# Four short-run transfers for the natural h, a new order of the first loads and constants, and a last norm by VectorE's statistics

## The chip, the cores and the metric

The kernel runs on one core of one Trainium2 chip. The metric is the device time of one execution in microseconds (us), lower is better. The names of the engines are those of the profile: PE is TensorE's matrix multiply, PEld its loading of weights (the stationary operand), DVE is VectorE, ACT is ScalarE, POOL is GpSimd, and SP is SyncE, the queue that issues nearly all DMA transfers here. All data is 32-bit float.

## What is computed

The input x holds 64 batches of 256 nodes with 128 channels; adj is a 256 x 256 symmetric-pattern matrix with values. Four graph layers follow each other; each one's result is added to its input and normalised over the channels.

```python
x = layernorm(x + chebyshev(x))            # layer 0: sum over k of A^k x W_k, k = 0..3, twice the same adj
x = layernorm(x + (adj @ (x @ W) + b))     # layer 1
x = layernorm(x + (A_norm @ x @ W.T + b))  # layer 2: A_norm = D^-1/2 (adj + I) D^-1/2
h = x
for step in range(5):                      # layer 3: a gated recurrent unit over the graph
    m = adj @ h                            # in_matrix and out_matrix are both adj here
    av = concat(m, m)
    u3 = h @ u3_w.T + u3_b
    z = sigmoid(av @ w3_w.T + w3_b + u3)
    r = sigmoid(av @ w4_w.T + w4_b + u3)
    hv = tanh(av @ w5_w.T + w5_b + ((r * h) @ u5_w.T + u5_b))
    h = (1 - z) * h + z * hv
x = layernorm(x + h)
```

## The kernel before

**Tiling.** The 64 batches are cut into 32 groups of two batches (`NB = 2`). One group's tensor is a tile of 128 partitions by 512 columns; its four node tiles (two batches of two tiles of 128 nodes) are the "q" of the code. A group runs through the four layers, and at most twelve groups are under way at once (`ACTIVE = 12`).

**Order.** Every piece of work is recorded as an `Op` with an engine, an assumed cost, a lag until others may use the result, and a rank. `Plan.order` simulates the engines with these figures and writes the instructions out in the order of the simulated start; an engine then runs its own list strictly in that order. Among pieces that could start at the same time the lower rank goes first. Pieces made by `pre` (loads, constants) have ranks written by hand; those of a group have the group's number as rank.

**Head.** `HEAD = 4`: groups that start below batch 4 (groups 0 and 1) are "near". A near group gets its transposed x by four PE transposes and one ACT copy (L867), multiplies by adj squared in the plain way (`propagate`, 8 PE instructions 256 columns wide) and uses `inner` (L584: 16 instructions of 256 columns, then 8 of 256). Every other group gets the transposed x by a DVE block transpose `tx` (L871), a store to DRAM and two loads back (L874, L879), uses `seven` (L723: seven block products instead of eight, 14 instructions of 128 columns, with sums and differences on POOL and DVE) and `inner_seven` (L618: 28 instructions of 128 columns, then 8 of 256). An fp32 product is two PE instructions.

**First loads and constants.** `a_nat` (adj), `w0_raw`, w1, and the six `raw_` weights are loaded on SP (L275, L306, L402, L407). PE transposes adj (L292), one ACT copy of 512 columns makes `aT` (L293), PE squares it, one ACT copy makes `a2T` (L303). The normalised adjacency `anT` comes by `degree`, a POOL power, `rows`, a PE transpose and `columns` (L369 to L373). `block_sums` (L378) makes five sums on DVE for each of `aT`, `a2T`, `anT` and `aTp`, where `aTp` is aT with its rows in another order (L345). From group 2 on, the load of a group's x waits for the first piece of work of the group two before it (`load_gate`, L956), until older gates take over.

**A step of layer 3** (L909 to L931). `seven` makes m from h with nodes on partitions ("natural"). PE then makes r, z and hv from m, from the transposed hT and from r * hT; ACT applies sigmoid and tanh; DVE makes the new hT. `packed` (L826) brings the natural h for the next step: one DVE block transpose (L830), one store of 256 KB to DRAM (L833) and two loads of 128 KB, one for each batch (L837). Its columns stand in pairs: the two node tiles' values for one channel lie side by side. `pairs` (L458) therefore gives `seven` a view with a stride of two elements, as PE's stationary operand and as POOL's input.

**End.** The last six batches (groups 29 to 31, `END = 6`) don't go through DRAM at the end: `closing` (L687) adds h and the residual in one PSUM bank, by products with `less` = I - 1/128 that also take out the mean. `spread_of` (L537) gets the mean square by four ACT squares with accumulation (L543), POOL takes the power -1/2 (L547), DVE multiplies (L704), and SP stores.

Of the kernel before, what the change touches and what calls it, by code (L numbers as in the profile page):

```python
# [14 lines left out]
P = 128  # L15
NB = 2
ACTIVE = 12
HEAD = 4
LEVEL = 7
# [158 lines left out]
def kernel(  # L178
# [105 lines left out]

    def flat(v):
        return v.ap.rearrange("p t n -> p (t n)")

    def turned_early():
# [3 lines left out]
    pre(-8, "PE", 8 * 110, turned_early, [a_nat], [p_at, warm])  # L292
    pre(-8, "ACT", act_cost(512), lambda: nc.scalar.copy(flat(aT), p_at.ap), [p_at], [aT])  # L293

# [7 lines left out]
    pre(-8, "PE", pe_cost(N, 4) + 220, square, [a_nat, aT], [p_a2, warm])  # L302
    pre(-8, "ACT", act_cost(512), lambda: nc.scalar.copy(flat(a2T), p_a2.ap), [p_a2], [a2T])  # L303

# [63 lines left out]

    pre(0.3, "DVE", 1500, degree, [a_nat], [ahat, deg])  # L369
    pre(0.3, "POOL", 700, lambda: nc.gpsimd.tensor_tensor(dinv.ap, deg.ap, half[:, :T], op=OP.pow), [deg], [dinv])  # L370
    pre(0.9, "DVE", 600, rows, [ahat, dinv, w0s], [ahat])
    pre(1.1, "PE", 4 * 110, lambda: turn(p_an, ahat), [ahat], [p_an])
    pre(0.3, "DVE", 900, columns, [p_an, dinv], [anT])  # L373

# [18 lines left out]
    block_sums(0.6, "a2T", a2T)  # L393
    block_sums(0.6, "anT", anT, (centred,))
    block_sums(0.7, "aTp", aTp, (centred,))

# [4 lines left out]
    made = pre(-7, "DVE", 100, lambda: nc.vector.tensor_copy(wb.ap[:, 1:3, 0], w0s.ap[:, :2, 0]), [w0s], [wb])  # L401
    fetch(0.6, wb.ap[:, 0, :], w1, wb, "SP")  # L402
    for i, b in ((1, b1), (2, b2)):
        last = fetch(0.5, wb.ap[:, i, :], bass.AP(tensor=b.tensor, offset=b.offset, ap=[[0, P], [1, C]]), wb, "POOL", (made,))
    pre(0.9, "DVE", 1100, lambda: centre(wb, wbm), [wb, w0s], [wb, wbm])
    w1c, b1c, b2c = ((wb, wb.ap[:, i, :]) for i in range(3))
    raw = {name: load(0.6, f"raw_{name}", [P, src.shape[1]], src, False, lag=9000)  # L407
           for name, src in (("w2", w2), ("w4", w4_w), ("w3", w3_w), ("w5", w5_w), ("u3", u3_w), ("u5", u5_w))}
    both = {name: Val("w", [P, C], f"both_{name}") for name in ("w4", "w3", "w5", "w34")}
    for name in ("w4", "w3", "w5"):  # L410
        pre(0.4, "DVE", 220, lambda o=both[name], i=raw[name]: nc.vector.tensor_add(  # L411
            o.ap, i.ap[:, :C], i.ap[:, C:]), [raw[name]], [both[name]])
    pre(0.4, "DVE", 220, lambda: nc.vector.tensor_sub(both["w34"].ap, both["w3"].ap, both["w4"].ap),
        [both["w3"], both["w4"]], [both["w34"]])
# [53 lines left out]
    class Group:  # L468
# [68 lines left out]
        def spread_of(self, tag, s):  # L537

            y, ve, rs = self.val("w", "y" + tag), self.val("ve", "ve" + tag), self.val("rs", "rs" + tag)

            def squares():
                for q in range(self.q):
                    nc.scalar.activation(nat(y)[:, q, :], nat(s)[:, q, :], AF.Square, scale=C ** -0.5,  # L543
                                         bias=root[:, 0:1], accum_out=ve.ap[:, q:q + 1])

            def scales():
                nc.gpsimd.tensor_tensor(rs.ap, ve.ap, half[:, :self.q], op=OP.pow)  # L547

            self.act(squares, [s], [y, ve], 390 * self.q)
            self.add("POOL", 1040, 100, scales, [ve], [rs])  # L550
            return y, rs

# [134 lines left out]
        def closing(self, y, hT, e, behind):  # L687
# [14 lines left out]
            self.pe(pe_cost(P, self.q), lambda: turned(e, False, True), [e, less], [s])  # L702
            o, rs = self.spread_of("3", s)
            self.dve(lambda: nc.vector.tensor_tensor(nat(o), nat(s), rs.ap[:, :, None].to_broadcast([P, self.q, C]),  # L704
# [121 lines left out]
        def packed(self, name, src):  # L826


            turn, far, t = self.val("w", "t" + name), self.val("dram", "d" + name), self.val("w", name)
            self.dve(lambda: nc.vector.transpose(  # L830
                turn.ap.rearrange("p (u j t) -> p u t j", t=T, j=32),
                src.ap.rearrange("p (u t i) -> p u t i", t=T, i=32)), [src], [turn])
            self.add("SP", 420, 2000, lambda: nc.sync.dma_start(far.ap, turn.ap), [turn], [far])  # L833

            def run():
                for b in range(self.nb):
                    nc.sync.dma_start(t.ap.rearrange("p (b r n) -> b p r n", b=self.nb, r=4)[b],  # L837
                                      far.ap.rearrange("(r i) (k b n) -> b (i k) r n", r=4, b=self.nb, k=4)[b])

            self.add("SP", 1000, 2300, run, [far], [t])  # L840
            return t
# [18 lines left out]
        def record(self):  # L860
            x_ = self.val("x", "x")
            plan.add("SP", 450, (6000, 9000)[self.start // NB] if self.start < HEAD else 2700, self.rank() - 1.5, lambda: nc.sync.dma_start(nat(x_), self.view(x)), [], [x_],
                     self.load_gate)
# [45 lines left out]
            for s in range(STEPS):  # L909
# [19 lines left out]
                if s < STEPS - 1:  # L929
                    hT = self.tensor(f"hT{s}", OP.add, hT, e)  # L930
                    h, ats, ins = self.packed(f"h{s}", hT), aTp, pairs  # L931
            if self.start < B - END:
# [13 lines left out]
    for i, nb in enumerate(sizes):  # L946
# [6 lines left out]
        if loaded:  # L953
            group.load_gate = (loaded[-1].last,)
        elif group.start >= HEAD:
            group.load_gate = (groups[i - 2].first,)  # L956
# [52 lines left out]
```

## Time and profile before

| | us |
|---|---|
| median of 3 runs (1341.92 to 1343.14) | 1342.21 |
| the profiled execution | 1342.32 |
| its span, first to last instruction | 1340.5 |
| PE busy | 1325.7 |
| DVE busy | 1039.0 |
| ACT busy | 773.6 |
| POOL busy | 636.1 |

The span is 1.8 us below the profiled execution's own time, and this execution stands 0.1 us above the median of the runs. Busy time is the union of an engine's instructions; since matmuls are pipelined and their ends are modelled, the rate of the PE is read from the distance of their starts, not from their durations. The granted TensorE clock is 0.997 of full speed on the mean over the span. "DMA" in the views by window is the mean busy share of the core's 16 DMA engines.

### The profile page before, as it was taken

What the parts mean: (1) busy time and instruction counts of PE and PEld (TensorE: products, weight loads), DVE (VectorE), ACT (ScalarE), POOL (GpSimd) and SP (SyncE); (2) the same over time, 40 slices, a digit from 0 to 9 for tenths busy, and PEclk for the clock granted to TensorE, in tenths of its full rate; (3) what the DMA queues carried; (4) which work ended last, traced back from release to release, by engine and by line L of the source; (5) the groups of instructions that cost most, each with busy time, mean ns of one, the idle gap of its engine ahead of it and who ended that gap; (6) DMA issues with size and microseconds to landing.
All of it is one profiled execution on the core that took longest, in us unless ns stands there. A gap on an engine that the chain in (4) does not pass through costs nothing.

```text
span 1340.5 us, 22669 instructions
## 1 busy us (share of the span) xinstructions
PE 1325.7 (99%) x6915; PEld 931.9 (70%) x6915; DVE 1039.0 (78%) x2577; ACT 773.6 (58%) x2361; POOL 636.1 (47%) x998
## 2 busy tenths in 40 slices
PE   8999999999999999999999999999999999999997
PEld 7987666667877766777766686777676776566554
DVE  7867767897778778788888797778876778777776
ACT  4587464645666664656655565655556786444445
POOL 5788352325646543447453454545345574232212
PEclk9999999999999999999999999999999999999999
DMA  7412333433433342333442343424322233333323
GB/s 190 131 33 79 88 95 87 141 107 96 115 95 111 95 121 70 110 95 103 121 124 74 108 134 87 119 71 119 101 73 68 60 111 103 112 109 95 89 85 103
DMA packets 269305, 134.87 MB, mean 101 GB/s; under 512 B 175712, under 2 KB 240864, under 8 KB 269184
## 3 DMA queue, kind: packets, MB, share of 16 engines
q1 hardware_dynamic: 268928, 133.29, 34.6%
q8 instruction: 55, 0.90, 0.3%
q0 software_dynamic: 256, 0.13, 0.1%
q14 instruction: 66, 0.54, 0.1%
HBM read 67.31 MB, written 65.80 MB: 99 GB/s over the span
## 4 chain that ended last, share of the span: by engine, by line
PE 97%; DVE 1%; DMA 1%; issue 0%; SPq 0%; ACT 0%; POOLq 0%; POOL 0%; ACTq 0%
PE pr L219 31%; PE ph L219 21%; PE pmg L219 19%; PE py L219 11%; PE pm L219 8%; PE pz L219 4%; PE pmq L219 3%; DMA x<-in_x_dram 1%; PE s L219 1%; DVE tx L871 0%; SPq L345 0%; DVE sd L635 0%; ACT y L543 0%; POOLq L1004 0%; DVE both_w L411 0%
## 5 line engine op out<-in xcount | busy, mean ns | idle before, releaser
L219 PE MATMUL pr<-mg,w435u5T 128*128 128x512 f32 x640 | 319.7, 593 | 0.0
L744 POOL TENSOR_TENSOR tsg<-h 128x256 f32<-128x256 f32 x128 | 94.0, 735 | 281.1 <-DMA h<-dh 200.4
L850 ACT ACTIVATE r<-pr,bsum 128x512 f32<-128x512 f32 x160 | 105.2, 658 | 123.4 <-PE pr L219 114.9
L850 ACT ACTIVATE pr<-pr,bsum 128x512 f32<-128x512 f32 x160 | 105.2, 658 | 118.0 <-PE pr L219 117.7
L547 POOL TENSOR_TENSOR rs<-ve,half 128x4 f32<-128x4 f32 x99 | 101.6, 1027 | 145.8 <-ACT y L543 137.2
L543 ACT ACTIVATE y<-s,root 128x128 f32<-128x128 f32 x396 | 153.7, 392 | 28.2 <-DVE s L565 25.5
L857 DVE TENSOR_TENSOR d<-ph,hT 128x512 f32<-128x512 f32 x160 | 109.6, 685 | 72.1 <-ACT ph L850 69.2
L219 PE MATMUL ph<-mg,w435u5T 128*128 128x512 f32 x320 | 163.3, 593 | 0.0
L219 PE MATMUL ph<-rh,w435u5T 128*128 128x512 f32 x320 | 162.7, 593 | 0.0
L219 PE MATMUL pr<-hT,w2u3T 128*128 128x512 f32 x320 | 162.2, 593 | 0.0
L219 PEld LDWEIGHTS pr<-mg,w435u5T 128*128 128x128 f32 x640 | 108.8, 191 | 70.3 <-issue 57.6
L850 ACT ACTIVATE ph<-ph,bsum 128x512 f32<-128x512 f32 x160 | 105.4, 659 | 57.8 <-PE ph L219 55.5
L219 PEld LDWEIGHTS pmg<-aTp,h 128*128 128x128 f32 x512 | 90.5, 196 | 64.8 <-issue 40.5
L857 DVE TENSOR_TENSOR rh<-r,hT 128x512 f32<-128x512 f32 x160 | 109.3, 683 | 33.1 <-ACT r L850 29.5
L558 ACT ACTIVATE y<-s,rs 128x128 f32<-128x128 f32 x384 | 122.1, 394 | 5.2 <-POOL rs L547 4.8
L857 DVE TENSOR_TENSOR pr<-pr,d 128x512 f32<-128x512 f32 x157 | 108.1, 691 | 1.7 <-ACT pr L850 0.5
L857 DVE TENSOR_TENSOR hT<-hT,pr 128x512 f32<-128x512 f32 x157 | 106.1, 678 | 1.3
L219 PE MATMUL pmg<-s_aTp,tsg 128*128 128x128 f32 x768 | 106.7, 275 | 0.0
L219 PEld LDWEIGHTS ph<-rh,w435u5T 128*128 128x128 f32 x320 | 58.5, 190 | 62.7 <-issue 46.2
L219 PE MATMUL pmg<-aTp,h 128*128 128x128 f32 x512 | 98.1, 279 | 0.0
L891 POOL TENSOR_TENSOR yb<-y,wb 128x512 f32<-128x512 f32 x64 | 81.7, 1277 | 34.3 <-ACT y L558 33.0
L780 DVE TENSOR_TENSOR mg<-pmg,usg 128x256 f32<-128x256 f32 x160 | 66.6, 418 | 39.7 <-PE pmg L219 38.3
(200 smaller groups left out, 2826.4 us busy)
## 6 DMA issues: line engine op xcount, KB each, us to landing
dh<-th SPq DMA_DIRECT2D x160, 256.0 KB, 2.0
h<-dh SPq DMA_DIRECT2D x256, 128.0 KB, 2.5
x<-in_x_dram SPq DMA_DIRECT2D x32, 256.0 KB, 3.2
hT<-dh SPq DMA_DIRECT2D x128, 64.0 KB, 2.1
out_dram<-y SPq DMA_DIRECT2D x32, 256.0 KB, 2.5
dx<-tx SPq DMA_DIRECT2D x30, 256.0 KB, 2.5
xT<-dx SPq DMA_DIRECT2D x60, 128.0 KB, 2.7
dn<-tn SPq DMA_DIRECT2D x29, 256.0 KB, 2.0
```

What stands on the lines that cost most here:

```text
L219: nc.tensor.matmul(o, lhsT, rhs, start=start, stop=stop, skip_group_check=shared)
L543: nc.scalar.activation(nat(y)[:, q, :], nat(s)[:, q, :], AF.Square, scale=C ** -0.5, bias=root[:, 0:1], accum_out=ve.ap[:, q:q + 1])
L547: nc.gpsimd.tensor_tensor(rs.ap, ve.ap, half[:, :self.q], op=OP.pow)
L558: nc.scalar.mul(nat(y)[:, q, :], nat(s)[:, q, :], rs.ap[:, q:q + 1])
L744: nc.gpsimd.tensor_tensor(ts.ap[:, :2 * P].rearrange("p (x c) -> p x c", x=2), ins(h)[:, 1], ins(h)[:, :, 0], op=OP.subtract)
L780: nc.vector.tensor_tensor(o(m, slice(1, 3)), o(ps, slice(1, 3), False), both, op=OP.add)
L850: self.act(lambda: nc.scalar.activation(t.ap, ps.ap, func, bias=bias[1], scale=1.0), [ps, bias[0]], [t], act_cost(self.width) + 100)
L857: self.dve(lambda: nc.vector.tensor_tensor(out(t), way(a), way(b), op=op), [a, b], [t])
L891: nc.gpsimd.tensor_tensor(nat(yb), nat(y), bias[1][:, None, :].to_broadcast([P, self.q, C]), op=OP.add)
```

## The change

The natural h of steps 1 to 4 is laid out with each node tile contiguous. The DVE transpose keeps plain 32-blocks, and `packed` loads by four transfers (one for each node tile q) with runs of 32 elements, 128 bytes, where it had two with runs of 64 elements. `seven` then gets `ins = None`, the contiguous view `tiles`.

`HEAD` becomes 6, so that group 2 is near too. The loads of x for groups 2 and 3 lose their gate, and have other assumed lags. The copies to `aT` and `a2T` are halved between ACT and DVE. `degree`, the power, `rows`, the turn, `columns`, the sums of `anT` and `aTp`, w1, the raw weights and the sums of w3, w4 and w5 get ranks from 1.9 to 2.6, where they had 0.3 to 1.1; `degree` now waits for `w0s`.

The last group (batches 62 and 63) gets its mean square by DVE: four `bn_stats`, four `bn_aggr` and one add, in place of the four ACT squares.

```diff
--- before.py
+++ after.py
@@ -15,7 +15,7 @@
 P = 128
 NB = 2
 ACTIVE = 12
-HEAD = 4
+HEAD = 6
 LEVEL = 7
 PLAIN = 0
 END = 6
@@ -282,15 +282,17 @@
                 nc.tensor.transpose(ps.ap[:, mt * N + nt * P:mt * N + (nt + 1) * P],
                                     src.ap[:, nt, mt * P:(mt + 1) * P], ident)
 
-    def flat(v):
-        return v.ap.rearrange("p t n -> p (t n)")
-
     def turned_early():
         turn(p_at, a_nat)
         warming(4)
 
     pre(-8, "PE", 8 * 110, turned_early, [a_nat], [p_at, warm])
-    pre(-8, "ACT", act_cost(512), lambda: nc.scalar.copy(flat(aT), p_at.ap), [p_at], [aT])
+    def halved(v, ps):
+
+        pre(-8, "ACT", act_cost(N), lambda: nc.scalar.copy(v.ap[:, 0, :], ps.ap[:, :N]), [ps], [v], joint=True)
+        pre(-8, "DVE", 420, lambda: nc.vector.tensor_copy(v.ap[:, 1, :], ps.ap[:, N:]), [ps], [v], joint=True)
+
+    halved(aT, p_at)
 
     def square():
         for mt in range(T):
@@ -300,7 +302,7 @@
         warming(2)
 
     pre(-8, "PE", pe_cost(N, 4) + 220, square, [a_nat, aT], [p_a2, warm])
-    pre(-8, "ACT", act_cost(512), lambda: nc.scalar.copy(flat(a2T), p_a2.ap), [p_a2], [a2T])
+    halved(a2T, p_a2)
 
 
     w0_raw = load(-1, "w0_raw", [P, C, K0], w0, lag=7300)
@@ -366,11 +368,11 @@
             nc.vector.tensor_scalar(anT.ap[:, mt, :], p_an.ap[:, mt * N:(mt + 1) * N], dinv.ap[:, mt:mt + 1],
                                     None, op0=OP.mult)
 
-    pre(0.3, "DVE", 1500, degree, [a_nat], [ahat, deg])
-    pre(0.3, "POOL", 700, lambda: nc.gpsimd.tensor_tensor(dinv.ap, deg.ap, half[:, :T], op=OP.pow), [deg], [dinv])
-    pre(0.9, "DVE", 600, rows, [ahat, dinv, w0s], [ahat])
-    pre(1.1, "PE", 4 * 110, lambda: turn(p_an, ahat), [ahat], [p_an])
-    pre(0.3, "DVE", 900, columns, [p_an, dinv], [anT])
+    pre(2.3, "DVE", 1700, degree, [a_nat, w0s], [ahat, deg])
+    pre(2.3, "POOL", 720, lambda: nc.gpsimd.tensor_tensor(dinv.ap, deg.ap, half[:, :T], op=OP.pow), [deg], [dinv])
+    pre(2.3, "DVE", 800, rows, [ahat, dinv], [ahat])
+    pre(2.3, "PE", 4 * 110, lambda: turn(p_an, ahat), [ahat], [p_an])
+    pre(2.3, "DVE", 900, columns, [p_an, dinv], [anT])
 
 
     sums_of = {}
@@ -391,26 +393,26 @@
 
     block_sums(0.6, "aT", aT)
     block_sums(0.6, "a2T", a2T)
-    block_sums(0.6, "anT", anT, (centred,))
-    block_sums(0.7, "aTp", aTp, (centred,))
+    block_sums(2.4, "anT", anT, (centred,))
+    block_sums(2.6, "aTp", aTp, (centred,))
 
 
 
     wb, wbm = constant("wb", [P, 3, C]), constant("wbm", [P, 3])
 
     made = pre(-7, "DVE", 100, lambda: nc.vector.tensor_copy(wb.ap[:, 1:3, 0], w0s.ap[:, :2, 0]), [w0s], [wb])
-    fetch(0.6, wb.ap[:, 0, :], w1, wb, "SP")
+    fetch(1.9, wb.ap[:, 0, :], w1, wb, "SP")
     for i, b in ((1, b1), (2, b2)):
         last = fetch(0.5, wb.ap[:, i, :], bass.AP(tensor=b.tensor, offset=b.offset, ap=[[0, P], [1, C]]), wb, "POOL", (made,))
     pre(0.9, "DVE", 1100, lambda: centre(wb, wbm), [wb, w0s], [wb, wbm])
     w1c, b1c, b2c = ((wb, wb.ap[:, i, :]) for i in range(3))
-    raw = {name: load(0.6, f"raw_{name}", [P, src.shape[1]], src, False, lag=9000)
+    raw = {name: load(2.0, f"raw_{name}", [P, src.shape[1]], src, False, lag=9000)
            for name, src in (("w2", w2), ("w4", w4_w), ("w3", w3_w), ("w5", w5_w), ("u3", u3_w), ("u5", u5_w))}
     both = {name: Val("w", [P, C], f"both_{name}") for name in ("w4", "w3", "w5", "w34")}
     for name in ("w4", "w3", "w5"):
-        pre(0.4, "DVE", 220, lambda o=both[name], i=raw[name]: nc.vector.tensor_add(
+        pre(2.0, "DVE", 300, lambda o=both[name], i=raw[name]: nc.vector.tensor_add(
             o.ap, i.ap[:, :C], i.ap[:, C:]), [raw[name]], [both[name]])
-    pre(0.4, "DVE", 220, lambda: nc.vector.tensor_sub(both["w34"].ap, both["w3"].ap, both["w4"].ap),
+    pre(2.0, "DVE", 300, lambda: nc.vector.tensor_sub(both["w34"].ap, both["w3"].ap, both["w4"].ap),
         [both["w3"], both["w4"]], [both["w34"]])
 
     less = constant("less", [P, P])
@@ -548,6 +550,23 @@
 
             self.act(squares, [s], [y, ve], 390 * self.q)
             self.add("POOL", 1040, 100, scales, [ve], [rs])
+            return y, rs
+
+        def spread_at_once(self, tag, s):
+
+            st, mv, ve, rs, y = (self.val(k, n + tag) for k, n in (
+                ("st", "st"), ("mv", "mv"), ("ve", "ve"), ("rs", "rs"), ("w", "y")))
+
+            def stats():
+                for q in range(self.q):
+                    nc.vector.bn_stats(st.ap[:, q * 6:(q + 1) * 6], nat(s)[:, q, :])
+                for q in range(self.q):
+                    nc.vector.bn_aggr(mv.ap[:, 2 * q:2 * q + 2], st.ap[:, q * 6:(q + 1) * 6])
+                nc.vector.tensor_scalar(ve.ap, mv.ap.rearrange("p (q k) -> p k q", k=2)[:, 1], EPS, None, op0=OP.add)
+
+            self.dve(stats, [s], [st, mv, ve], 260 * self.q + 110)
+            self.add("POOL", 1040, 100, lambda: nc.gpsimd.tensor_tensor(rs.ap, ve.ap, half[:, :self.q], op=OP.pow),
+                     [ve], [rs])
             return y, rs
 
         def normalise_centred(self, tag, s):
@@ -700,7 +719,7 @@
 
             self.pe(pe_cost(P, self.q) + pe_cost(self.width), early, [hc, y, less], [s], behind=(behind,))
             self.pe(pe_cost(P, self.q), lambda: turned(e, False, True), [e, less], [s])
-            o, rs = self.spread_of("3", s)
+            o, rs = (self.spread_at_once if self.start >= B - NB else self.spread_of)("3", s)
             self.dve(lambda: nc.vector.tensor_tensor(nat(o), nat(s), rs.ap[:, :, None].to_broadcast([P, self.q, C]),
                                                      op=OP.mult), [s, rs], [o])
             return o
@@ -827,17 +846,17 @@
 
 
             turn, far, t = self.val("w", "t" + name), self.val("dram", "d" + name), self.val("w", name)
-            self.dve(lambda: nc.vector.transpose(
-                turn.ap.rearrange("p (u j t) -> p u t j", t=T, j=32),
-                src.ap.rearrange("p (u t i) -> p u t i", t=T, i=32)), [src], [turn])
+            self.dve(lambda: nc.vector.transpose(turn.ap.rearrange("p (u j) -> p u j", j=32),
+                                                 src.ap.rearrange("p (u i) -> p u i", i=32)), [src], [turn])
             self.add("SP", 420, 2000, lambda: nc.sync.dma_start(far.ap, turn.ap), [turn], [far])
 
             def run():
-                for b in range(self.nb):
-                    nc.sync.dma_start(t.ap.rearrange("p (b r n) -> b p r n", b=self.nb, r=4)[b],
-                                      far.ap.rearrange("(r i) (k b n) -> b (i k) r n", r=4, b=self.nb, k=4)[b])
-
-            self.add("SP", 1000, 2300, run, [far], [t])
+                f = far.ap.rearrange("(r i) (k q j) -> q (i k) r j", r=4, q=self.q, k=4)
+                o = t.ap.rearrange("p (q r j) -> q p r j", q=self.q, r=4)
+                for q in range(self.q):
+                    nc.sync.dma_start(o[q], f[q])
+
+            self.add("SP", 450 * self.q, 2300, run, [far], [t])
             return t
 
         def product(self, ps, w, rhs, start, stop, shared=False):
@@ -859,7 +878,7 @@
 
         def record(self):
             x_ = self.val("x", "x")
-            plan.add("SP", 450, (6000, 9000)[self.start // NB] if self.start < HEAD else 2700, self.rank() - 1.5, lambda: nc.sync.dma_start(nat(x_), self.view(x)), [], [x_],
+            plan.add("SP", 450, dict(zip(range(0, 4 * NB, NB), (6000, 9000, 10500, 9000))).get(self.start, 2700), self.rank() - 1.5, lambda: nc.sync.dma_start(nat(x_), self.view(x)), [], [x_],
                      self.load_gate)
 
             near = self.start < HEAD
@@ -928,7 +947,7 @@
                 e = self.tensor(f"e{s}", OP.mult, z, d, into=pr)
                 if s < STEPS - 1:
                     hT = self.tensor(f"hT{s}", OP.add, hT, e)
-                    h, ats, ins = self.packed(f"h{s}", hT), aTp, pairs
+                    h, ats, ins = self.packed(f"h{s}", hT), aTp, None
             if self.start < B - END:
                 hT = self.tensor("hT", OP.add, hT, e)
                 hn = self.brought("hn", self.turned("n", hT, "p (k q i) -> p q k i", "p (k q j) -> p q k j"))
@@ -952,7 +971,7 @@
             group.gate = (done[-1].last,)
         if loaded:
             group.load_gate = (loaded[-1].last,)
-        elif group.start >= HEAD:
+        elif group.start >= 4 * NB:
             group.load_gate = (groups[i - 2].first,)
         group.record()
         groups.append(group)
```

## The prediction

> **What bounds the kernel now.** I read the page first: which engine is full, and what the transfers cost.
>
> ```profile
> PE 1325.7 (99%) x6915; PEld 931.9 (70%) x6915; DVE 1039.0 (78%) x2577; ACT 773.6 (58%) x2361; POOL 636.1 (47%) x998
> ...
> q1 hardware_dynamic: 268928, 133.29, 34.6%
> ...
> h<-dh SPq DMA_DIRECT2D x256, 128.0 KB, 2.5
> ...
> hn<-dn SPq DMA_DIRECT2D x116, 64.0 KB, 2.0
> ```
>
> PE is busy for all but 15 us of a span of 1340.5; DVE, ACT, POOL and the DMA engines have room. So time is saved only by less PE work, faster PE work, or fewer of those 15 us. The busy time by windows shows where they lie (columns: window, then busy us and instructions of PE, PEld, DVE, ACT, POOL, then granted clock, DMA share, GB/s).
>
> ```profile
> 25.00:30.00 5.00, 2.95 (x25) 2.72 (x23) 3.58 (x7) 3.42 (x15) 4.44 (x7) 1.00 0.93 255
> 30.00:35.00 5.00, 1.93 (x9) 1.93 (x10) 4.83 (x12) 0.68 (x3) 1.26 (x2) 0.61 0.82 230
> 35.00:40.00 5.00, 4.64 (x31) 4.35 (x31) 3.44 (x12) 1.98 (x8) 0.87 (x1) 0.71 0.76 204
> 40.00:50.00 10.00, 8.98 (x73) 8.59 (x72) 9.20 (x23) 3.86 (x16) 7.89 (x13) 1.00 0.02 4
> 50.00:60.00 10.00, 10.00 (x83) 9.73 (x83) 9.38 (x23) 7.93 (x34) 8.31 (x12) 1.00 0.90 254
> ...
> 120.00:600.00 480.00, 480.00 (x2451) 329.99 (x2450) 372.53 (x917) 271.72 (x802) 221.84 (x353) 1.00 0.35 101
> ```
>
> PE idles 2.05 + 3.07 + 0.36 + 1.02 = 6.5 us between 25 and 50, and never from 50 to 1330. The clock column adds a second loss: after the stall PE runs at about half speed from 33.07 to 38.0, where it is busy 1.93 + 2.64 = 4.6 us; half of that, 2.3 us, is lost. The hole is worth 8.8 us. The rest is start-up (PE begins real work at 4 us) and the 7 us after the last matmul. PE's waits (who waited for whom: us in total, times, longest) and then DVE's timeline (start us, duration us, instruction, idle before) name the cause.
>
> ```profile
> PE pmq L219 <- DVE mq L776: 5.1, 1, 5.1
> ...
> PE pz L219 <- DVE u L664: 1.0, 1, 1.0
> ```
>
> These and two waits at 1.4 and 0.4 us are all that PE has in the whole run. What DVE did meanwhile:
>
> ```profile
> 26.11 1.13 DVE L871 STREAM_TRANSPOSE tx<-x 128x512 f32<-128x512 f32 x1 [1.79 <-DMA x<-in_x_dram]
> 27.17 0.82 DVE L366 TENSOR_SCALAR anT<-p_an,dinv 128x256 f32<-128x256 f32 x2
> 28.27 1.08 DVE L871 STREAM_TRANSPOSE tx<-x 128x512 f32<-128x512 f32 x1 [0.28 <-DMA x<-in_x_dram]
> ...
> 29.77 1.65 DVE L385 TENSOR_TENSOR s_anT<-anT 128x128 f32<-128x128 f32 x1
> ...
> 31.67 0.28 DVE L770 TENSOR_TENSOR usq<-usq,pmq 128x128 f32<-128x128 f32 x1
> ```
>
> DVE works in order. From 24.3 it waits for a gated x, then transposes two x, makes anT and its sums, and only at 31.67 reaches the short additions for group 2's `pmq`, whose last product PE can't write before. Early constants and late x stand ahead of what PE needs.
>
> **What the Trainium skill says.** "TensorE: Matmul & The Clock Gate", section "What's actually happening": an idle window of about 3.4 us throttles the PE clock to half, and it takes about as long of work to come back. The trace agrees: 5.1 us idle, then 0.61 and 0.71 granted. The same page, "LDWEIGHTS (loading the stationary operand)", gives columns / 1.2, 107 ns for 128; the trace's products of 128 columns start 111.7 ns apart, so these are bound by their loads. "SBUF — State Buffer", "Door 1: The DMA port swizzle", says that an fp32 stride up to a 16-byte line is free; a stride of two elements should then cost nothing. The trace differs (PE timeline):
>
> ```profile
> 1267.45 0.40 PE L219 MATMUL pmg<-aTp,h 128*128 128x128 f32 x2
> 1267.68 0.83 PE L219 MATMUL pmg<-s_aTp,tsg 128*128 128x128 f32 x6
> 1268.35 0.40 PE L219 MATMUL pmg<-aTp,h 128*128 128x128 f32 x2
> ```
>
> The strided h takes 0.23 / 2 = 115 ns for each, the contiguous tsg 0.67 / 6 = 112. Over 60 to 1300 us the starts in the trace lie 115.4 ns apart on the mean after a strided h, 111.7 after tsg or tqg. The measurement decides: 3.7 ns for each.
>
> **The change part by part.**
>
> (a) *Contiguous h as weights.* The groups pmg<-aTp,h (x512) and pmg<-s_aTp,h (x256) are 768 products in steps 1 to 4. 768 x 3.7 ns = **-2.8 us**, all on PE and so all on the path. Bounds: 0 if the difference isn't the stride's; -4.6 if the 6 ns between the medians of the durations (281 against 275) counts. POOL gains nothing: its first difference takes 732 ns from strided h and 731 from contiguous y. Nor does the DVE transpose: 704 ns in `packed`, 702 and 704 in `turned`, which moves whole blocks.
>
> (b) *Four transfers for two.* 128 x 2 more issues on SP at about 0.45 us each: 115 us more on a queue that now issues some 860 transfers (390 us, 29% of the span), giving 38%. SP has room, but h comes later: two issues take 0.91 us, the four of `hn` 1.75, so +0.84 us for each step. From issue to POOL's use is 3.0 us now (1278.40 to 1281.38), and a step's chain is some 17.5 us: POOL 1.9, `seven` about 3, two ACT gates 1.3, six DVE pieces 4.1, PE in between 1.7, store 2.3, loads 3.0. Two groups of PE work, 2 x 6.6 us, cover 13 of this, three cover 20; up to twelve are under way, so it is hidden but for the last steps. I take 0, and 0 to +2 as bounds for the end. Packets: 131072 of 256 bytes become 262144 of 128. The trace's records give 17.9 ns on the mean for a 256-byte packet. "DMA: Bandwidth & Descriptors", "Why small descriptors are slow (HBM only)", has 3 cycles on top of one for 32 bytes, 11 for 256 bytes and 7 for 128: estimate 11.4 ns each, which the trace doesn't show. The DMA engines then get 40 us more each (the share 38%), at most 147 us (46%) if a packet costs the same. No bound either way.
>
> (c) *Group 2 near.* PE gets more work: four transposes, 4 x 0.112 = 0.45; `propagate` 8 x 0.216 against 14 x 0.112, +0.16; `inner` 24 x 0.216 = 5.18 against 28 x 0.112 + 8 x 0.216 = 4.86, +0.32. Sum **+0.9 us**, certain. (0.216 is the distance of the starts of 256-column products.) It takes `tx`, its store and two loads, the differences and the short additions off POOL, DVE and SP: on DVE 1.1 + 1.7 + 1.1 + 1.6 = 5.5 us, just where DVE is late. And PE gets 7.3 us of work that needs only ACT.
>
> (d) *Order of loads and constants.* x of groups 2 and 3 now goes out ungated after the fourth SP issue, at about 3 to 4 us, ahead of aTp, w1 and the raw weights (now 10.4 us and later). Group 3's tx can run at about 10 us instead of 20.8; DVE then doesn't meet a missing x. w1 and the six raws issue behind aTp, about 11 to 14 us, land 4 to 5 us later; the first use of w1 is near 25 us, later for the others. DVE gives up about 1.6 us of `degree` before 5.4 us and some 9 us of anT, its and aTp's sums and the raw sums between 12 and 32; they come back beside groups 0 to 3, where `inner` needs no DVE. PE's supply from 8.5 us: three near groups, 3 x 7.3 = 22 us, so to about 31; then group 3 (6.4) and layer 1 of groups 0 to 2 (2.5 each), to about 45. DVE must do in 15 to 45 some 8 us of constants, 17 for three DMA groups, 5 for layer 1: 30 of 30 us. It just fits, so I don't take the whole hole: of 8.8 us I take **-7.0**, with 1.8 left as short waits without a cold clock. Bounds: 0 and -8.8.
>
> (e) *Halved copies.* An ACT copy of 512 columns takes 0.59 us, of 256 0.37; a DVE piece from PSUM of 256 columns 0.41 to 0.42. DVE is free at both places once `degree` is gone. 2 x 0.17 = **-0.3**, if x and w0s don't hold PE instead (w0s was done at 12.9, behind the sums of a2T).
>
> (f) *The last norm.* The tail's timeline:
>
> ```profile
> 1331.61 1.95 PE L219 MATMUL s<-less,e 128*128 128x128 f32 x16
> ...
> 1334.29 1.01 POOL L547 TENSOR_TENSOR rs<-ve,half 128x4 f32<-128x4 f32 x1 [3.50 <-ACT y L543]
> ...
> 1335.69 1.01 POOL L547 TENSOR_TENSOR rs<-ve,half 128x4 f32<-128x4 f32 x1 [0.39 <-ACT y L543]
> ```
>
> ACT squares group 30 until 1334.2 and group 31 until 1335.6. DVE would start group 31 at 1333.6: four bn_stats 0.87 (start of the first to end of the last, L519), four bn_aggr 0.4, the add 0.17: ready at 1335.0. POOL is then taken by group 30's power until 1335.3, so the second starts 0.35 us earlier: **-0.35**. If bn_stats from PSUM costs 0.07 more each, still -0.3; bounds 0 and -0.4.
>
> Sum: -2.8 + 0 + 0.9 - 7.0 - 0.3 - 0.35 = -9.5. 1342.3 - 9.5 = 1332.8, against the profiled execution's 1342.32, which is the runs' median within 0.1.
>
> **The rivals.**
>
> *The hole moves instead of closing.* The constants that are put later meet DVE, POOL and SP at 25 to 50 us, where DVE was already 92% busy in 40 to 50. For it: DVE's 30 of 30. Against it: from 50 to 120 us DVE carried 72 to 94% and PE waited for nothing. If only a quarter of the hole goes, -2.2 for -7.0: 1337.6.
>
> *Slower, by late h.* Each of 128 steps has 0.84 us more between store and use. For it: the h issued at 1278.40 has its last difference ready at 1283.18, and PE takes its first product at 1283.22, with no slack. Against it: POOL waits 200 us in all for h, and PE waits for nothing after 50 us. The gains must be eaten first: 9.5 + 2.7 for slower by 0.2%, that is 12.2 / 0.84, about 15 of 128 steps with the whole delay on PE, most likely in the last three groups' four steps each plus gaps that the clock makes dearer. At 16 steps: 1332.8 + 13.4 = 1346.2.
>
> *The stride isn't the cause* of the 3.7 ns: (a) is nothing and the time is 1335.6. This lies inside the forecast's range.
>
> **How the numbers follow.** Forecast (hole mostly closed, with or without the stride's gain) 0.70, the moved hole 0.18, late h 0.12. The forecast's own range is 1329.5 (the whole hole, a stride at 4.6) to 1336. 0.2% of 1342 is 2.7 us, about what a measurement can tell from no change: faster below 1339.5, slower above 1344.9. Faster: 0.70 + 0.14 of the moved hole = 0.84; same: 0.04 of it and 0.02 of the late h, 0.06; slower 0.10. The range for 8 in 10 must take in most of the moved hole: 1329 to 1339.
>
> **What would show it.** (a): medians of the pmg<-aTp,h loads at 192 ns and matmuls at 275, starts 112 apart. (b): h<-dh x512 of 64 KB, packets near 400,000, and PE's waits from 50 to 1330 still near nothing. (c): twelve `ptx` transposes where there are eight, and 24 products of 256 columns on `pmq<-a2T,x` where there are 16. (d): no PE wait over 2 us between 25 and 50 and a clock of 1.00 there. (e): p_a square starting about 0.2 us after p_at less than now. (f): the last power on POOL right behind the one before. A wait of PE on DMA-fed POOL work after 1250 us, or a throttled window, would prove me wrong.

## The result and the profile after

The changed kernel takes 1335.93 us (median of 5 runs, 1335.43 to 1336.32) where the kernel before takes 1342.21 (5 runs beside them): ratio 0.9952, 95% interval 0.9939 to 0.9966, 6.3 us less. The profiled execution took 1335.43 with a span of 1333.5; 6.9 us below the profiled execution of before, of which the steps are counted here. The forecast was 1332.8, inside the range of 1329 to 1339 and the right way, but with half as much gain again as there was (9.5 for 6.3).

The page after, engines, queue and the loads of h:

```profile
PE 1321.0 (99%) x6901; PEld 925.1 (69%) x6901; DVE 1037.3 (78%) x2574; ACT 774.3 (58%) x2355; POOL 632.7 (47%) x995
...
q1 hardware_dynamic: 402896, 132.78, 39.5%
...
h<-dh SPq DMA_DIRECT2D x512, 64.0 KB, 2.4
```

There are 134,000 packets more for the same bytes, and the DMA share is up from 34.6 to 39.5%: inside the bounds of 38 and 46%. PE still bounds the kernel. Busy time by windows after (columns as before):

```profile
25.00:30.00 5.00, 5.00 (x30) 4.51 (x29) 2.56 (x3) 3.85 (x17) 4.17 (x6) 1.00 0.83 233
30.00:35.00 5.00, 4.94 (x37) 4.55 (x35) 4.18 (x6) 4.06 (x16) 3.18 (x5) 1.00 0.90 236
35.00:40.00 5.00, 2.78 (x21) 2.50 (x22) 5.00 (x17) 2.53 (x10) 3.91 (x6) 1.00 0.89 240
40.00:50.00 10.00, 9.15 (x82) 8.99 (x81) 9.20 (x28) 5.19 (x24) 8.48 (x13) 1.00 0.61 162
50.00:60.00 10.00, 9.79 (x80) 9.42 (x80) 10.00 (x27) 4.86 (x22) 8.69 (x13) 1.00 0.30 79
...
120.00:600.00 480.00, 479.51 (x2479) 330.43 (x2478) 387.35 (x950) 279.17 (x836) 225.50 (x355) 1.00 0.42 105
```

The 5 us hole at 28 to 33 is gone, and so is the half clock behind it: it reads 1.00 in each of these windows. A smaller hole stands at 35 to 38. PE's waits and DVE's timeline after name it:

```profile
PE pmq L219 <- ACT usq L805: 1.9, 1, 1.9
...
PE pm L219 <- DVE m L795: 1.2, 2, 0.8
PE pmg L219 <- DVE mg L795: 0.5, 1, 0.5
```

```profile
30.23 1.11 DVE L890 STREAM_TRANSPOSE tx<-x 128x512 f32<-128x512 f32 x1 [2.12 <-DMA x<-in_x_dram]
31.27 0.82 DVE L368 TENSOR_SCALAR anT<-p_an,dinv 128x256 f32<-128x256 f32 x2
32.65 1.12 DVE L890 STREAM_TRANSPOSE tx<-x 128x512 f32<-128x512 f32 x1 [0.56 <-DMA x<-in_x_dram]
33.71 1.13 DVE L385 TENSOR_TENSOR s_anT<-anT 128x128 f32<-128x128 f32 x1
34.87 0.70 DVE L386 TENSOR_TENSOR s_anT<-s_anT,anT 128x128 f32<-128x128 f32 x1
...
36.03 0.27 DVE L789 TENSOR_TENSOR us<-us,pm 128x128 f32<-128x128 f32 x1
```

It is the same picture as before, some 4 us later and with the x of later groups: DVE waits for a late x, transposes it, makes anT and its sums, and only at 36.03 reaches the short addition. Two of the sums take 1.13 and 0.70 us where their like takes 0.28; POOL's additions run beside them. ACT's copy of `usq` stands behind ACT's `m`, which comes only after that addition, and PE waits for the copy. PE's timeline after shows the products on h:

```profile
1260.72 0.39 PE L219 MATMUL pmg<-aTp,h 128*128 128x128 f32 x2
1260.94 0.83 PE L219 MATMUL pmg<-s_aTp,tsg 128*128 128x128 f32 x6
1261.61 0.39 PE L219 MATMUL pmg<-aTp,h 128*128 128x128 f32 x2
```

Two products on h now take 0.22 us from start to start and not 0.23: the mean over all 768 is 111.0 ns, where it was 115.4. The tail after:

```profile
1328.33 1.01 POOL L568 TENSOR_TENSOR rs<-ve,half 128x4 f32<-128x4 f32 x1
1328.39 0.69 DVE L723 TENSOR_TENSOR y<-s,rs 128x512 f32<-128x512 f32 x1 [0.36 <-POOL rs L549]
1329.11 1.35 SPq L958 DMA_DIRECT2D out_dram<-y  x2
1329.37 0.69 DVE L723 TENSOR_TENSOR y<-s,rs 128x512 f32<-128x512 f32 x1 [0.28 <-POOL rs L568]
```

The last product starts at 1326.35 and the last power 1.98 us later, where it was 2.40 (1333.29 and 1335.69).

### The profile page after: what moved, and what is told of

It is laid out like the page before. It is cut to its first block, busy times and chain, and to the rows that moved or that the text cites. A ratio compares the mean times of both kernels' runs of the same rounds, so it can differ in the third digit from the quotient of the medians.

```text
span 1333.5 us, 23248 instructions
## 1 busy us (share of the span) xinstructions
PE 1321.0 (99%) x6901; PEld 925.1 (69%) x6901; DVE 1037.3 (78%) x2574; ACT 774.3 (58%) x2355; POOL 632.7 (47%) x995
## 3 DMA queue, kind: packets, MB, share of 16 engines
q1 hardware_dynamic: 402896, 132.78, 39.5%
## 4 chain that ended last, share of the span: by engine, by line
PE 96%; DVE 3%; DMA 1%; ACT 0%; issue 0%; POOL 0%; POOLq 0%; DVEq 0%; ACTq 0%; SPq 0%
PE pr L219 31%; PE ph L219 20%; PE pmg L219 19%; PE py L219 11%; PE pm L219 7%; PE pz L219 4%; PE pmq L219 3%; DMA x<-in_x_dram 1%; PE s L219 1%; DVE tx L890 0%; PE warm L270 0%; ACT y L545 0%; DVE se L660 0%; DVE sf L663 0%; DVE sd L654 0%
## 5 line engine op out<-in xcount | busy, mean ns | idle before, releaser
L219 PEld LDWEIGHTS pmg<-aTp,h 128*128 128x128 f32 x512 | 86.7, 191 | 60.7 <-issue 38.4
L219 PEld LDWEIGHTS pmg<-s_aTp,tsg 128*128 128x128 f32 x768 | 96.0, 192 | 0.0
```

The lines of the kernel that those rows point to most:

```text
L219: nc.tensor.matmul(o, lhsT, rhs, start=start, stop=stop, skip_group_check=shared)
```

## The experiments

Each kernel was run in five rounds beside the kernel before, whose median was 1342.3 to 1342.7. "Lost" is worked out from the traces: the sum, over PE's products, of the distance to the next start less 112, 216 or 430 ns for 128, 256 or 512 columns. After 120 us only gaps of more than 0.03 us over that are counted, so the stride isn't in it. Before, e2_split and e3_tail have the same order and the same front, and differ by 0.9 us at 25 to 80 and by nothing after 120: smaller differences in the third column mean nothing.

| kernel | ratio to before, 95% interval | lost at 25 to 80 us | lost after 120 us |
|---|---|---|---|
| before | 1 | 9.6 | 0.7 |
| changed | 0.9952 (0.9939 to 0.9966) | 4.7 | 0.9 |
| e1_layout | 0.9988 (0.9981 to 0.9994) | 9.8 | 1.9 |
| e2_split | 1.0005 (0.9997 to 1.0014) | 9.9 | 0.7 |
| e3_tail | 0.9997 (0.9989 to 1.0005) | 9.0 | 0.7 |
| e4_front | 0.9942 (0.9929 to 0.9954) | 0.4 | 1.5 |
| e5_order | 0.9969 (0.9958 to 0.9979) | 0.4 | 7.4 |
| e6_seed | 0.9953 (0.9941 to 0.9966) | 4.9 | 1.7 |
| e7_head4 | 0.9948 (0.9936 to 0.9961) | 3.6 | 1.3 |
| e8_ranks | 0.9940 (0.9928 to 0.9952) | 2.2 | 3.6 |
| e9_pin7 | 0.9956 (0.9943 to 0.9968) | 0.4 | 6.1 |
| e10_before0 | 1.0014 (1.0007 to 1.0020) | 8.1 | 2.9 |
| e11_xonly | 1.0023 (1.0014 to 1.0031) | 10.2 | 3.7 |
| e12_e4split | 0.9974 (0.9964 to 0.9984) | 0.4 | 4.8 |

### The layout, the transfers and the norm, each alone

e1_layout is the kernel before with the new `packed`, its SP figure left at 1000 so that every instruction keeps its place:

```diff
+                for q in range(self.q):
+                    nc.sync.dma_start(o[q], f[q])
...
             self.add("SP", 1000, 2300, run, [far], [t])
...
-                    h, ats, ins = self.packed(f"h{s}", hT), aTp, pairs
+                    h, ats, ins = self.packed(f"h{s}", hT), aTp, None
```

> The kernel before with the natural h contiguous and its four loads alone; every instruction in the order of before. My theory (a product on strided h weights starts 3.7 ns later, 768 of them; the later h is hidden): 2.8 us less than before, 1339.4, starts after h at 111.7 ns, PE waits as before. Rival, late h: the 0.84 us more for each step show as PE waits, and the time is at or above 1342.2. Rival, the stride is not the cause: starts stay at 115.4 ns and the time at 1342.2.

1340.71 us against 1342.7; the ratio says 1.6 us less, 0.8 to 2.6. The slower starts come with the stride: they go with it here, and stay in e2_split, below, which keeps it. The view of tile h (columns: count, then least, median and largest ns, first and last start), in the kernel before:

```profile
L219 PEld LDWEIGHTS pmg<-aTp,h x512: 192/196/200, 113.5 to 1315.3; 128*128 128x128 f32 x171
L219 PE MATMUL pmg<-aTp,h x512: 272/281/283, 113.6 to 1315.5; 128*128 128x128 f32 x171
```

and in e1_layout:

```profile
L219 PEld LDWEIGHTS pmg<-aTp,h x512: 186/190/192, 113.1 to 1312.9; 128*128 128x128 f32 x171
L219 PE MATMUL pmg<-aTp,h x512: 272/275/275, 113.2 to 1313.0; 128*128 128x128 f32 x171
```

The loads went from 196 to 190 ns, the starts from 115.4 to 111.1: 768 x 4.3 ns = 3.3 us, even more than forecast. But part came back: lost after 120 us rose by 1.2. The later issue alone doesn't explain this, for e2_split has it in the same order and loses no more than before; the 128-byte runs or a faster PE that waits for the same work are left, and no run parts them. The median is neither theory's, though the profiled execution took 1339.86.

e2_split keeps the paired h and cuts each load in two:

```diff
-                    nc.sync.dma_start(t.ap.rearrange("p (b r n) -> b p r n", b=self.nb, r=4)[b],
-                                      far.ap.rearrange("(r i) (k b n) -> b (i k) r n", r=4, b=self.nb, k=4)[b])
+                    o = t.ap.rearrange("p (b r n) -> b p r n", b=self.nb, r=4)[b]
+                    f = far.ap.rearrange("(r i) (k b n) -> b (i k) r n", r=4, b=self.nb, k=4)[b]
+                    for g in range(2):
+                        nc.sync.dma_start(o[:, 2 * g:2 * g + 2], f[:, 2 * g:2 * g + 2])
```

> The kernel before with the paired h kept, but each of its two loads cut into two of 64 KB (runs of 256 bytes as before); order as before. My theory: 1342.2 within 0.5 us, since the later h is hidden behind other groups' products, and starts after h stay at 115.4 ns. Rival, late h: PE waits appear, most of them after 1250 us, and the time is 1343 to 1350.

1343.62 us against 1342.7, an interval that holds no change. The median itself lies in the rival's range, but the rival's waits aren't there: starts stay at 115.4, PE has no new wait, and 0.7 us are lost after 120 as before. In the order of before, four issues cost nothing that shows.

e3_tail gives the kernel before the new last norm:

```diff
-            o, rs = self.spread_of("3", s)
+            o, rs = (self.spread_at_once if self.start >= B - NB else self.spread_of)("3", s)
```

> The kernel before with the last group's mean square by VectorE alone. My theory: the last power starts 0.35 to 0.4 us earlier after the last product, but the trace of the changed kernel shows the stores' end moving by only 0.1 us: time 1341.8 to 1342.1, span after the last product's start 6.8 to 7.2 us where it was 7.2. Rival, the store follows: 1341.8 or less, with the interval clear of no change.

Too small for the timing (ratio 0.9997 with 1 inside). In its profile the end stands 6.84 us after the last product's start, before 7.24: 0.4, at the short end of this theory's range and as the forecast had it. Over all the traces it is 6.84 to 7.15 us in the seven kernels with the new norm (mean 7.06) and 7.23 to 7.76 in the seven with the old one (7.39).

### The front alone, and the order that the planner draws

e4_front is the changed kernel with the old `packed`, `pairs` and last norm.

> The changed kernel with the paired h and its two loads and with the old last norm: what is left is group 2 near, the order of loads and constants and the halved copies. My theory: 6.3 less 2.8 and 0.1 leaves 3.4 us, time about 1338.8, with the hole at 25 to 60 us as in the changed kernel (3.5 us idle). Rival, the stride gives nothing and the front gives all: 1336.

1334.65 us: both numbers missed, and it is no slower than the whole change. Its hole is closed. Windows of e4_front:

```profile
25.00:50.00 25.00, 25.00 (x195) 23.82 (x194) 22.41 (x56) 16.43 (x64) 20.46 (x28) 1.00 0.66 177
50.00:80.00 30.00, 30.00 (x229) 28.23 (x228) 23.80 (x60) 25.20 (x110) 26.65 (x38) 1.00 0.31 89
...
120.00:600.00 480.00, 479.64 (x2426) 327.56 (x2425) 381.41 (x933) 275.06 (x815) 217.85 (x346) 1.00 0.36 104
```

The edits that bear on the first 80 us are the same in both kernels, yet one loses 0.4 us there and the other 4.7. What differs is the draw: the planner tries twelve orders with random additions to the ranks and takes that with the shortest simulated end. With `packed` at 1000 it is the eighth, as in the kernel before; with 1800 it is the first, drawn without additions. PE's orders part at 21.6 us, after 94 instructions. e5_order puts this to the test:

```diff
-            self.add("SP", 450 * self.q, 2300, run, [far], [t])
+            self.add("SP", 1000, 2300, run, [far], [t])
```

> The changed kernel with one figure of the planner left as before: the assumed SP cost of the natural h's loads is 1000, not 1800. Its instructions then stand in the order of e4_front, not in that of the changed kernel. My theory (the 4 us that the changed kernel still loses at 25 to 50 us belong to the order that the planner picked, not to the edits): hole under 1 us, and 2.8 for the stride, 0.4 for the last norm less about 1 for late loads come on top of e4_front: 1331.5 to 1332.5. Rival, the four loads of 128-byte runs cost what e4_front had gained: 1334.5 to 1336.

1338.35 us, beyond both ranges. The first half of the theory held (0.4 lost at 25 to 80), the second failed: with PE's order that of e4_front, 7.4 us are lost after 120. Windows of e5_order:

```profile
120.00:600.00 480.00, 476.49 (x2418) 324.29 (x2417) 381.98 (x931) 272.69 (x807) 217.39 (x345) 1.00 0.41 103
```

Its longest wait, by timeline, PE, then DVE and SP:

```profile
310.13 0.46 PE L219 MATMUL pmg<-s_aTp,h 128*128 128x128 f32 x2 [1.69 <-issue]
```

```profile
309.40 0.43 DVE L654 TENSOR_TENSOR sd<-xT 128x256 f32<-128x256 f32 x1 [2.26 <-DMA xT<-dx]
309.75 0.28 DVE L795 TENSOR_TENSOR mg<-wsg,pmg 128x128 f32<-128x128 f32 x1
```

```profile
302.98 2.02 SPq L857 DMA_DIRECT2D h<-dh  x4
305.11 0.99 SPq L898 DMA_DIRECT2D xT<-dx  x2
```

The same pieces in e4_front's timeline:

```profile
307.86 0.42 DVE L654 TENSOR_TENSOR sd<-xT 128x256 f32<-128x256 f32 x1
308.19 0.28 DVE L795 TENSOR_TENSOR mg<-wsg,pmg 128x128 f32<-128x128 f32 x1
```

```profile
301.90 0.93 SPq L856 DMA_DIRECT2D h<-dh  x2
302.94 0.99 SPq L898 DMA_DIRECT2D xT<-dx  x2
```

The profile names no releaser here ("issue"). In the code this product is the `rest` of `seven`, which may write `pmg` only after DVE's `mg` (L795) has read it; that addition ends at 310.03 and PE starts 0.1 us later. The addition stands in DVE's queue behind `sd`, which waits 2.26 us for the transposed x of another group, in layer 0. That x is late because its two loads stand in SP's queue behind the h: they go out at 305.11, where e4_front has them at 302.94, half of it from the later h (302.98 for 301.90) and half from its two more issues. So the work that PE misses isn't that of the late h: three queues in order, SP's, DVE's and PE's, carry the delay to another group and back. e12_e4split parts the later issue from the 128-byte runs, with the edit of e2_split made in e4_front:

> e4_front in its own order, with the paired h, but each of the two loads of h cut into two of 64 KB with 256-byte runs: four issues, packets as before. It parts the two causes of e5_order's 7 us idle after 120 us. If the 0.8 us later issue does it: 4 us or more idle after 120 and 1338 or more. If the 128-byte runs do it (landing 2.4 us where these land in 2.1): under 2.5 us idle, and within 1 us of e4_front's 1334.7.

1339.08 us, 4.8 lost after 120, with the 64 KB transfers landing in 2.1 us: the later issue alone costs 3.3 us (4.8 less 1.5) in this order. Its longest wait is the same one, and again `mg` stands behind the x:

```profile
309.23 0.54 DVE L654 TENSOR_TENSOR sd<-xT 128x256 f32<-128x256 f32 x1 [1.60 <-DMA xT<-dx]
309.69 0.28 DVE L795 TENSOR_TENSOR mg<-wsg,pmg 128x128 f32<-128x128 f32 x1
```

PE goes on at 310.06, right behind it. What the other 2.6 us of e5_order are isn't shown. Its 128-byte runs land in 2.4 us, but its PE is also faster, and that counts: into this wait PE came from a product begun at 308.16 in e5_order and at 308.65 in e12_e4split, and left it at 310.13 and 310.06, so that nearly all of the 0.6 us more that e5_order loses here is PE's own gain, waited away. So e2_split's nothing held for one order only.

e9_pin7 leaves every figure of the changed kernel, 1800 too, but takes the eighth order:

```diff
-        for _ in range(tries):
+        for n in range(tries):
...
-                if best is None or span < best[0]:
+                if best is None or n == 7:
```

> The changed kernel, every edit and figure as it is, but of the planner's twelve trial orders the eighth is used (the one that e4_front and e5_order have) and not the first; up to PE row 300, some 100 us, it is e4_front's order, and after that the late h is planned with 1800. My theory (the changed kernel's hole is its draw of order; e5_order's stalls after 120 us are h that comes later than planned): loss under 1 us at 25 to 80 us, under 2.5 idle after 120, time 1331.5 to 1333.5. Rival, four loads of 128-byte runs stall any order: 5 us or more idle after 120 and 1336 or more.

1336.49 us. The hole is closed again (0.4), which shows with e4_front and e5_order that the changed kernel's remaining hole belongs to its draw. Not all 4.3 us are gained by it: in this order PE's wait for `w0s` at 12 to 13 us is 1.0 us (0.9 in e4_front and e5_order), where the changed kernel has 0.4. But 6.0 us are lost between 600 and 1200, so the time is outside both expectations. The largest of these waits isn't a late h. Timeline of e9_pin7, DVE and then POOL:

```profile
742.55 1.94 DVE L657 TENSOR_TENSOR ss<-xT,mq 128x256 f32<-128x256 f32 x2
744.41 2.08 DVE L660 TENSOR_TENSOR se<-ss,xT 128x256 f32<-128x256 f32 x2
...
750.08 0.67 DVE L876 TENSOR_TENSOR rh<-r,hT 128x512 f32<-128x512 f32 x1
```

```profile
742.76 1.45 POOL L910 TENSOR_TENSOR yb<-y,wb 128x512 f32<-128x512 f32 x1
744.16 0.64 POOL L770 TENSOR_TENSOR tq<-ts,y 128x128 f32<-128x128 f32 x1
744.76 1.45 POOL L910 TENSOR_TENSOR yb<-y,wb 128x512 f32<-128x512 f32 x1
```

Each of these DVE additions takes about 1 us beside POOL's additions, where the median of L657 in this run is 0.417; the r * h product comes late by them, and PE waits 1.8 us for it. Whether 1800 hides the late h in general stays open: in the changed kernel's order it does (0.9 lost), here other things stall.

e6_seed has the changed kernel's edits and the planner's seed 2:

> The changed kernel with another seed for the planner's random ranks, nothing else. My theory (order luck): the loss at 25 to 60 us differs from the changed kernel's 4.7 by more than 1 us in one direction or the other, the time is 1332 to 1339. Rival, the loss belongs to the edits: 1335.9 within 0.7.

1336.26 us, 4.9 lost at 25 to 80 against 4.7. By its own number the expectation failed and the rival's is met, though the loss now lies in other places (0.7 at 33, 0.8 at 44, 1.3 at 48). The draw decides in e4_front, e5_order and e9_pin7; not every draw differs.

### Which edit closes the hole

e7_head4 is e5_order with `HEAD = 4`; e8_ranks is e5_order with the old ranks for the constants; e11_xonly is the kernel before with the new gate and lags of x alone (eighth order), e10_before0 the kernel before in its first order.

```diff
-        elif group.start >= HEAD:
+        elif group.start >= 4 * NB:
```

> e5_order with group 2 not near (HEAD = 4), its x and group 3's still loaded early. My theory (group 2 near is what takes work off VectorE while it is late): the hole comes back by 3 us or more, 0.9 us of PE work goes: 1334 or more. Rival, the order of loads and constants alone closes the hole: 1331, 0.9 less than e5_order.

> e5_order with the ranks of the constants (anT, sums of anT and aTp, w1, raw weights and their sums) as before; group 2 near and the early x stay. My theory (constants ahead of the short additions were one of two causes): 2 to 4 us of hole come back, 1334 to 1336. Rival, the missing x was the only cause: within 0.7 us of e5_order.

> The kernel before with only the loads of x for groups 2 and 3 ungated (and their assumed lags), eighth trial order. My theory after e7_head4 and e8_ranks, which each lost only 2 to 4 us at 25 to 80 without one of the other two edits (the early x is the edit that the hole needs most): loss falls from 9.6 to 5 us or less, time 1338 or less. Rival, it needs group 2 near or the later constants too: 8 us or more lost, 1341 or more.

> The kernel before with the first of its twelve trial orders in place of the eighth. My theory (early constants and late x make the hole in any order, the draw only sizes it): 5 to 12 us lost at 25 to 80 us, time 1339 to 1346. Rival, the 9 us of before were only its draw: 4 us or less lost there, time 1337 to 1339.

e7_head4: 1335.16 us, 3.6 lost, 3.2 more than e5_order: as expected, though e5_order wasn't the 1332 that the times were set against. e8_ranks: 1334.28 us, 2.2 lost, 1.8 more, a little under what was expected. But neither keeps e5_order's draw: with these edits the planner's own figures make it choose the fifth of its twelve orders in e7_head4 and the second in e8_ranks. All the edits together lose 0.4 us in one draw and 4.7 and 4.9 in others, so 3.2 and 1.8 can't be put down to the edit that is missing. e11_xonly: my theory fell. 10.2 lost, and 1345.77 us. Windows of e11_xonly:

```profile
25.00:50.00 25.00, 18.99 (x137) 17.86 (x136) 21.93 (x55) 9.72 (x40) 16.93 (x24) 0.86 0.75 201
```

PE idles 6.0 us there and the clock drops to 0.86, as before. An x that is there early isn't enough while DVE has the constants and group 2's transposes and additions at once; with either of the other two edits beside it, each in the one order that was run, most of the hole goes. What each of the three is worth stays open, and whether group 2 near and later constants would do without the early x wasn't tried. e10_before0: 8.1 lost, so the hole of before isn't an accident of its draw alone. What is shown is the whole: 8.1 to 10.2 us are lost in three orders without the edits together, 0.4 to 4.9 in three with them. Both other orders of the old work (e10 and e11) lose 2.9 and 3.7 us after 120 where the kept order loses 0.7: an order is worth some 2 to 3 us there with nothing changed in the work.

## Why the prediction was right or wrong

Its reading of the bound held: what was gained is PE's, and nearly all of it came from the two places named, the strided h and the hole. By its own parts, against the profiled executions (-9.5 forecast, -6.9 measured):

- **(a) Contiguous h**: -2.8 forecast; the starts give 768 x 4.3 ns = -3.3, and waits after 120 us rose by 0.2. Right, a little small; POOL (729 ns for 732) and DVE gained nothing, as said. The pace is 111 ns in every kernel with the contiguous h and 115.3 to 115.4 in every one with the strided h, whatever the order. That products of 128 columns are bound by their loads isn't shown: those of 256 and 512 columns start 216 and 430 ns apart, and by the half of 216, 108 ns, the product itself would take about as long.
- **(b) Four transfers**: 0 forecast, and in the changed kernel's order 0.2. The reason given, that groups under way cover it, is not right in general: the later issue cost nothing in e2_split but 3.3 us in e12_e4split, and its waits lie mostly between 300 and 600 us with many groups under way, not in the last steps. The prediction counted the 0.84 us on the step's own chain and the four issues as room on SP. The largest wait came by another way: the issues put back another group's x on SP, and DVE's queue stood still for it. The chance of 0.12 for late h was low for a mechanism that takes 3.3 us back in one order.
- **(c) Group 2 near**: +0.9 of PE work, there: the trace after has 24 more instructions of 256 columns and 38 fewer of 128, 24 x 0.216 - 38 x 0.112 = 0.9.
- **(d) Order of loads and constants**: this is the step that failed in size. -7.0 was taken, "with 1.8 left as short waits without a cold clock". From the starts, the loss at 25 to 80 (9.6, where the prediction counted 8.8) went to 4.7: -4.9. The clock did stay at 1.00, but one wait of 1.9 us and three shorter ones (1.4 together) remain, for the very reason the prediction gave for the old hole. "It just fits" was a sum of DVE's work over 30 us, at each piece's usual duration; what counts is which instruction stands before which, and that a draw decides. Four kernels with the same front edits and the eighth draw (e4_front, e5_order, e9_pin7, e12_e4split) lose 0.4. The forecast knew of no draw, so it is partly luck that it came as near as it did.
- **(e) Halved copies**: -0.3 forecast. The first copy gave nothing (PE squares from 5.69 us, for 5.72), the second 0.2 (0.87 us from the last start of the square to the first product on a2T, for 1.05). DVE's half doesn't run beside ACT's, it waits for it, as the changed kernel's DVE timeline shows; why isn't known. And what PE gained went into a wait of 0.42 us at 12.89 for w0s, the case that the prediction had set as the exception.

```profile
5.49 0.42 DVE L293 COPY aT<-p_at 128x256 f32<-128x256 f32 x1 [3.91 <-ACT aT L292]
```

- **(f) Last norm**: -0.35 forecast. The power came 0.42 us earlier, the end of the span only 0.1 (7.15 us after the last product's start, for 7.24): from the last DVE piece to the end it took 3.4 us where it had been 3.1. In e3_tail the 0.4 arrived whole, so the remainder lies in the store, whose length varies between executions. The means over all the traces, 7.06 and 7.39, are 0.33 apart: right.

The rival of the moved hole had the right shape (DVE full, x late, constants in front): it would leave 6.6 us of hole and the forecast 1.8, and 4.7 were left, between the two. One slip of arithmetic: the forecast's own low end, by its parts, is 1329.2 and not 1329.5. The 0.6 us between 6.9 and 6.3 is the profiled execution being the fastest of its five.

No version here is shown to be faster than the changed kernel: e4_front and e8_ranks stand at 0.9942 and 0.9940 with intervals that overlap its own.

## What to carry to other kernels

Where a planner or a heuristic writes the order, an edit brings its own effect and a new draw: hold the order (an assumed figure or a fixed draw is enough) before an edit is credited with the time. Here a draw moved the loss at one place by up to 4 us, and the whole time by 0.3 and 0.6 us for the changed kernel (e6_seed, e9_pin7) and by some 2 for the one before (e10_before0). A transfer made later, or in more pieces, is hidden only as far as the in-order queues behind it were written for its new arrival, and the issuing queue is one of them; averages of idle time and the count of groups under way don't show that. On an engine that is busy 99% of the time, look at the distance of the starts by kind of operand: 4 ns on 768 instructions was the one change of pace that showed in every order.

## What the runs showed of the hardware

- An fp32 stationary operand with a stride of two elements costs 4.3 ns on the mean for each load and product of 128 columns (115.4 ns from start to start in the kernel before and 111.1 in e1_layout), where the Trainium skill ("SBUF — State Buffer", "Door 1: The DMA port swizzle") lets one expect none.
- A 128-byte packet takes 12.9 ns on the mean in e1_layout's records, a 256-byte packet 17.9; the prediction's estimate was 11.4. A load of 64 KB lands in 2.4 us with 128-byte runs and in 2.1 with 256-byte runs (e1_layout and e2_split).
- The Trainium skill, "SBUF — State Buffer", "Who interferes with whom", says that a DVE instruction with two SBUF inputs contends with a GpSimd instruction that reads SBUF. The traces agree, and it was dearer than I had expected: DVE additions of 0.42 us took about 1 us beside POOL's in e9_pin7, and the sum of anT at 29.77 us in the kernel before took 1.65 us for its usual 0.28 while POOL ran a power and two differences. The order's figures don't have this cost.
- The first products of the square, 256 columns wide, start 427 ns apart and later ones 216. The step between the two comes where the trace's record of the full clock begins, at 5.9 to 7.3 us, and differs by 1.4 us between kernels whose PE order is the same (5.92 in e1_layout, 7.34 in e3_tail). A gain of 0.3 us in the first microseconds can't be read from one execution's end.
